# Four layers of graph network on one core: the second attention step's propagation two tile pairs at a time, and two reorderings in layer 0

## The chip, the cores and the metric

The kernel runs on one core of a Trainium2 chip. The metric is the device time of one execution in microseconds; lower is better. A core has a matrix engine (TensorE, PE in the profile, with PEld for its weight loads), VectorE (DVE), ScalarE (ACT), GpSimd (POOL) and SyncE (SP), which here issues most of the transfers between main memory and the on-chip memory. All engines run side by side, each through its own queue in order, and wait for one another on semaphores. TensorE reads the on-chip memory and writes accumulators (PSUM), from which VectorE and ScalarE copy.

## The reference

A graph of 3327 nodes with 256 features passes four residual layers. Cut to what matters:

```python
h = relu(layernorm(x)); x = x + adj @ (h @ W.T + b)                  # layer 0
h = relu(layernorm(x)); x = x + relu(filtered(adj) @ (tanh(h @ Wp + bp) @ Wg) + bg)   # layer 1
h = relu(layernorm(x)); x = x + relu(A_norm @ (h @ W.T))             # layer 2, A_norm from adj + I
h = relu(layernorm(x))                                               # layer 3
R = (adj + I) / rowsum;  Z = 0;  Xf = Xa = h
for n in range(2):
    A  = top_p_attention(Xa)      # softmax(q k^T), kept up to mass 0.9 in each row, renormalized
    Xf = R @ Xf                   # propagation
    Xa = A @ Xa                   # attention
    Z  = Z + Xf @ U1[n].T + Xa @ U2[n].T
x = x + layernorm(h + Z) * g + b
```

In layer 1, `filtered` is tanh of adj times adj where adj is positive (the reference keeps the 700 largest of a row; the kernel counts the positives and has a second path for rows with more). All arithmetic is float32.

## The kernel before

The nodes are padded to 26 tiles of 128 (T = 26, H = 13). Tile m of the lower half has a partner m + 13 in the upper half; the two are a *pair*. Each product with the adjacency matrix is done by a scheme with seven half-size products in place of eight: the matrix is seen as four quadrants of 13 x 13 tiles, and sums of quadrants (some kept in `s_dram` from layer 0 or 2) are multiplied with sums of blocks of the right side (`ts`, made by `combine_nodes` or `combine` on VectorE). The products are numbered 1 to 7; each takes 13 matmuls for a tile pair, and the results are added up to the four quarters of the pair's rows.

Layer 0 makes one pair at a time (`products`, `Product`): 91 matmuls with the matrix tile as the standing operand, then `Product.result` adds up. That needs one copy by ScalarE (L699) and six additions by VectorE (L705 to L710); the last of them sets the accumulator free. Layers 1 and 2 make two pairs at a time (`doubles`, `Double`): the right side stands, and the two tiles' matrix blocks stream through, 256 columns at a time. A double keeps two accumulator tiles (tag `row`, two buffers in all), so the first double of layer 1 needs the tile of layer 0's last pair. `Feed` loads matrix slabs and, on VectorE, makes the sums of quadrants; in layer 1 each slab is filtered first by `filtered` (on VectorE and ScalarE, for every fourth slab on ScalarE alone: L925, L926, L927).

When a pair of layer 0 is done, `finish0` makes its rows of x1 and stores them, and a `Pair` of layer 1 normalizes them (`measure`, `apply`), has TensorE transpose them (`turn`) and multiplies them by the weights (`hidden`). These steps are hung as hooks between the matmuls of the next pair; for the last pair, between those of the first double, at its matmuls 36 and 48 of 91.

The first rows of the kernel (`first_two_in`) are normalized while the input arrives. VectorE, ScalarE and SP are ordered by hand there: pairs 0 and 1 are measured, pair 0 applied, pair 2 measured, pair 1 applied, and so on.

Layer 3 goes by tiles. For each tile, the logits (`logits_steps`, L1233) go from the `row` accumulators through ScalarE's exponential (L1258) into a row of 3328 scores; VectorE and ScalarE search the threshold (`search_steps`: two passes on ScalarE, L1291 and L1296, and on VectorE L1301 to L1346, of which L1307 and L1344 are passes over all 3328 scores), and TensorE multiplies the masked row with the values (`rows_times_steps`: 26 transposes L223, copied by ScalarE at L226, and 26 matmuls L234). The search runs three tiles ahead (AHEAD = 3). Between two attentions TensorE runs a part of the propagation. In the first step these parts are doubles of four phases (`FirstPropagation`, products (1, 2), (5, 4), (6, 3), (7)). In the second step, after the tile pair (0, 13), they are the two phases of a pair (`PropagatedPair`): products 1, 2, 5, 4 and then 6, 7, 3, with the matrix block standing and 128 columns of the right side streaming (L1559). The outcome has nodes on the partitions, as the rows of the output need. `half` copies the first accumulator on ScalarE, `whole` does five additions on VectorE (L1579 to L1586), and `finish_pair` makes the output rows of both tiles: loads of `z`, `u` and `x3`, adds on POOL, the layer norm on VectorE with its root on POOL (L123, L125), three more adds on POOL. Their stores are issued during the next pair. The last pair, tiles 12 and 25, ends the kernel by `finish3` and `finish_last`, in which product 3 of tile 12 comes last.

TensorE's order is the order of the program. For the other engines a planner sorts the instructions at build time by its own estimates, within the dependencies; `tc.high_priority()` puts work ahead, and `tc.issue_after(x)` puts a block's instructions of x's engine behind x. In layer 3, `plan` says after which matmul of the phase (counted in 26ths) other work of TensorE is put in: the logits at 7, the transposes that begin the next attention at 20.

## Time and profile before

| what | us |
|---|---|
| time, median of 3 runs (2452.27 to 2454.14) | 2453.4 |
| the profiled execution: time, span | 2453.7, 2451.7 |
| TensorE busy (matmul), of the span | 2435.4 (99%) |
| TensorE weight loads busy | 2108.2 (86%) |
| VectorE busy | 2053.3 (84%) |
| ScalarE, POOL busy | 1112.3, 289.9 |
| layer 3's second attention step | about 1735 to 2442 |

A line of the groups gives the program line, the engine, the operation, out<-in by the program's names, the shape, the count, then the busy time of the group, the mean of one in ns, and the idle time of the engine before it with what ended it. Lines of the order of time begin with the start in us and the duration; a run of equal instructions is one line with its count. In the windows, each engine has its busy time and the number of its instructions.

A matmul's record is longer than the distance to the next, because matmuls are pipelined; the distance between starts is what a run of them costs.

### The profile page before, as it was taken

Reading aid. Unit: us, or ns where it says so; the run is one execution under the profiler, and the core shown is the slowest. Engines: PE = TensorE matmul, PEld = TensorE weight load, DVE = VectorE, ACT = ScalarE, POOL = GpSimd, SP = SyncE. Lnnn points to the kernel's source line nnn. Section 1 sums busy time; section 2 is a strip of 40 time slices with the busy share of each in tenths; the row PEclk is TensorE's granted clock in tenths of the full one; section 3 lists DMA queues with packets and bytes.
Section 4 is the critical chain, followed back from the end, with each engine's and each line's share of the span. In section 5 each row is a group of like instructions: output and inputs, shape, how many; then the busy total and the mean of one; then the engine's idle time right before and its main releaser. Section 6 shows DMA issues by size and latency. Waiting matters only on the chain. (4 is left out here: it accounts for less than half of the span.)

```text
span 2451.7 us, 41088 instructions
## 1 busy us (share of the span) xinstructions
PE 2435.4 (99%) x14475; PEld 2108.2 (86%) x14475; DVE 2053.3 (84%) x5280; ACT 1112.3 (45%) x2141; POOL 289.9 (12%) x462
## 2 busy tenths in 40 slices
PE   9999999999999999999999999999999999999998
PEld 8999988889888897777787778778888888888887
DVE  7877798788867768889788787985999999999995
ACT  3000045564011126656556565654556555655551
POOL 2000010000000100000000100000213222222222
PEclk9999999999999999999999999999999999999999
DMA  6788856566978666322332323333534433444343
GB/s 208 248 272 272 289 178 182 179 199 188 296 238 268 201 196 189 118 80 84 108 105 80 97 86 110 92 92 121 164 97 138 146 116 116 135 139 132 116 130 123
DMA packets 278674, 387.79 MB, mean 158 GB/s; under 512 B 24253, under 2 KB 216250, under 8 KB 278458
## 3 DMA queue, kind: packets, MB, share of 16 engines
q1 hardware_dynamic: 257322, 367.54, 48.3%
q10 hardware_dynamic: 21136, 17.52, 2.2%
q8 instruction: 116, 1.90, 0.3%
q14 instruction: 100, 0.82, 0.1%
HBM read 315.37 MB, written 67.89 MB: 156 GB/s over the span
## 5 line engine op out<-in xcount | busy, mean ns | idle before, releaser
L226 ACT COPY eT_a<-pt_a 128x512 f32<-128x512 f32 (+1 forms) x364 | 187.0, 557 | 366.6 <-PE pt_a L223 362.7
L234 PE MATMUL a<-h3a,eT_a 128*128 128x256 f32 x1352 | 311.7, 379 | 0.2 <-ACT eT_a L226 0.2
L234 PE MATMUL a<-vs,eT_a 128*128 128x256 f32 x1352 | 309.1, 379 | 0.2 <-ACT eT_a L226 0.2
L1320 DVE MAX8 cand_a<-w 128x8 f32<-128x128 f32 x1352 | 284.8, 278 | 4.0
L234 PEld LDWEIGHTS a<-h3a,eT_a 128*128 128x128 f32 x1352 | 249.5, 189 | 44.7 <-issue 10.1
L234 PEld LDWEIGHTS a<-vs,eT_a 128*128 128x128 f32 x1352 | 248.9, 190 | 30.1 <-ACT eT_a L226 0.5
L1316 DVE SCALAR_TENSOR_TENSOR w<-e_a,t_a 128x896 f32<-128x896 f32 x208 | 230.0, 1106 | 3.4
L1258 ACT ACTIVATE e_a<-pl_a 128x1024 f32<-128x1024 f32 x260 | 184.4, 729 | 37.2 <-PE pl_a L1233 36.8
L1307 DVE SCALAR_TENSOR_TENSOR w<-e_a,t_a 128x3328 uint8<-128x3328 f32 x52 | 192.0, 3692 | 4.6 <-DVE t_a L1304 0.5
L1344 DVE SCALAR_TENSOR_TENSOR e_a<-e_a,all_least 128x3328 f32<-128x3328 f32 x50 | 184.4, 3688 | 1.7
L223 PE MATMUL pt_a<-ident,e_a 128*128 128x128 f32 x1352 | 181.4, 272 | 0.0
L223 PEld LDWEIGHTS pt_a<-ident,e_a 128*128 128x128 f32 x1352 | 159.9, 141 | 19.1 <-issue 0.4
L777 PE MATMUL acc_a<-s_a,tsa 128*128 128x256 f32 (+1 forms) x728 | 169.0, 364 | 1.8 <-DVE y_a L710 1.8
L777 PE MATMUL acc_a<-a_a,tsa 128*128 128x256 f32 (+1 forms) x728 | 169.3, 365 | 0.0
L1500 PE MATMUL f0a<-slab3a_0a,tsa 128*128 128x256 f32 (+1 forms) x728 | 161.4, 367 | 0.3 <-DMA slab3a_0a<-s_dram 0.3
L1291 ACT ACTIVATE junk_a<-e_a,t_a 128x3328 uint8<-128x3328 f32 x52 | 159.7, 3071 | 0.5
L777 PE MATMUL acc_a<-a_a,rhs 128*128 128x256 f32 (+1 forms) x728 | 158.2, 364 | 0.0
L1296 ACT ACTIVATE junk_a<-e_a,t_a 128x3328 uint8<-128x3328 f32 x50 | 153.3, 3066 | 0.0
L1559 PE MATMUL f1a<-tsa,slab3a_1a 128*128 128x128 f32 x1248 | 148.1, 276 | 0.0
L777 PEld LDWEIGHTS acc_a<-s_a,tsa 128*128 128x128 f32 x728 | 130.6, 190 | 18.1 <-ACT a_a L927 2.2
L1559 PEld LDWEIGHTS f1a<-tsa,slab3a_1a 128*128 128x128 f32 x1248 | 144.0, 192 | 1.8
L1500 PEld LDWEIGHTS f0a<-slab3a_0a,tsa 128*128 128x128 f32 x728 | 126.7, 190 | 20.0 <-issue 3.8
(286 smaller groups left out, 4313.3 us busy)
## 6 DMA issues: line engine op xcount, KB each, us to landing
a_a<-in_adj_t_dram SPq DMA_DIRECT2D x216, 256.0 KB, 3.5
a_a<-in_adj_t_dram SPq DMA_DIRECT2D x144, 384.0 KB, 4.1
slab3a_0a<-s_dram SPq DMA_DIRECT2D x95, 384.0 KB, 4.0
slab3a_0a<-in_adj_t_dram SPq DMA_DIRECT2D x65, 384.0 KB, 4.0
slab3a_1a<-s_dram SPq DMA_DIRECT2D x60, 384.0 KB, 4.0
a_a<-in_adj_t_dram SPq DMA_DIRECT2D x60, 320.0 KB, 4.4
slab3a_1a<-in_adj_t_dram SPq DMA_DIRECT2D x48, 384.0 KB, 4.0
s_dram<-s_a SPq DMA_DIRECT2D x45, 256.0 KB, 4.4
```

Source lines behind the costliest of these rows:

```text
L223: nc.tensor.transpose(pt[:, j, :], e[:, k * P : (k + 1) * P], ident)
L226: last_turned.append(nc.scalar.copy(eT[:, : len(blocks), :], pt[:, : len(blocks), :]))
L234: nc.tensor.matmul(acc[:, :width], ready[g][:, j, :], rhs[:, k, :], start=(k == 0), stop=(k == T - 1))
L777: nc.tensor.matmul(self.acc[n], t, slab[:, :, k - cuts(self.many)[c][0], :], start=(k == 0 and n in (1, 5, 6, 7)), stop=(k == H - 1 and n ...
L1258: last_exp.append(nc.scalar.activation(dst, src, AF.Exp, accum_out=parts[:, c : c + 1]))
L1291: nc.scalar.activation(junk_a, e, AF.Relu, scale=-1.0, bias=t, accum_out=short)
L1307: nc.vector.scalar_tensor_tensor(junk, e, t, e, ALU.is_lt, ALU.mult, accum_out=got)
L1316: nc.vector.scalar_tensor_tensor(w[:, : (b - a) * P], eg, t, eg, ALU.is_lt, ALU.mult, accum_out=below[:, g : g + 1])
L1320: nc.vector.max(cand[:, 8 * k : 8 * k + 8], w[:, (k - a) * P : (k - a + 1) * P])
L1344: nc.vector.scalar_tensor_tensor(e, e, least, e, ALU.is_ge, ALU.mult, accum_out=kept)
L1500: nc.tensor.matmul(self.acc[:, self.at[n]], right_half(h3, ts, n, k), self.block(phase, at), start=not at, stop=at == len(units) - 1, skip ...
L1559: nc.tensor.matmul(self.accs[bank][:, c * P : (c + 1) * P], self.block(phase, at)[:, 0, :], right_half(self.h, self.ts, n, k), start=start ...
```

## The change

1. **Second step's propagation.** `PropagatedPair` goes; `SecondPropagation`, a subclass of `FirstPropagation`, takes its place for tiles 1 to 12 and 14 to 25: six doubles (tiles 1 and 2 with 14 and 15, and so on) of four phases, one behind each of four attentions. The attention order is now 0, 13, then 1, 2, 14, 15, 3, 4, 16, 17, ... The right side stands and 256 columns stream. The outcome has features on the partitions, so `turned` lets TensorE transpose it back, four transposes for two tiles, into a `row` accumulator, which VectorE reads directly (`rows`). `finish_two` replaces `finish_pair` and `finish_last`: it ends two tiles of the same half at a time. The lower two are begun (loads, POOL adds) in the third phase at 14 and turned in the fourth at 4; the upper two are begun in the next double's first phase at 4 and turned at 14. Stores are issued at 2 of a phase. In the short fourth phase (13 matmuls) the logits stand at 14 and the next attention's beginning at 22.
2. **The last double.** Its lower tiles 11 and 12 are turned and ended during the last attention. Product 7 of the upper tiles is made last with the matrix block standing, so that its outcome needs no turning: tile 25 first, then tile 24. All else of these tiles is turned and added before.
3. **Seam of layers 0 and 1.** For the last pair of layer 0 the second `combine_nodes` comes behind the six additions and the row sums. `finish0`, `measure` and `apply` of that pair move from there to matmul 10 of the first double, with its store, and lose their priority; `turn` moves from 36 to 44 and `hidden` from 48 to 56. ScalarE's filter of the fourth slab of the second group is put behind the copy L699. In layer 1's first double two further combinations are put behind the additions.
4. **First rows.** Pair 1 is applied before pair 2 is measured.

`xa` tiles get four buffers instead of two. The diff, cut to its core:

```diff
-                        self.change(s, (i, j) == QUADS[-1])
+                        with tc.issue_after(copied[-1].ins) if (p, c, i, j) == (0, 1, *QUADS[-1]) else nullcontext():
+                            self.change(s, (i, j) == QUADS[-1])
...
-                    if p == H - 1 and c:
-                        combine_nodes(following, *CUTS[c - 1])
+                    if p == H - 1 and c == 1:
+                        combine_nodes(following, *CUTS[0])
...
-                with tc.high_priority() if p == H - 1 else nullcontext():
-                    finish(p, x2, y, p3)
-                    pair = pair_after(p, x2)
+                row_sums(p, p3)
+                if p == H - 1:
+                    with tc.issue_after(summed_up[-1].ins):
+                        combine_nodes(following, *CUTS[1])
+                    made = []
+
+                    def last():
+                        finish(p, x2, y)
+                        made.append(pair_after(p, x2))
+
+                    return [last, lambda: made[0].turn(), lambda: made[0].hidden()]
...
                 pairs[0].apply()
+                pairs[1].apply()
                 pairs[2].measure()
-                pairs[1].apply()
...
-                finish1, left, (36, 48), ((26, 36), (14, 20)), second_layer, following=rhs2,
+                finish1, left, (10, 44, 56), ((26, 36), (14, 20)), second_layer, following=rhs2,
...
+        class SecondPropagation(FirstPropagation):
+            def __init__(self, d):
+                super().__init__(d)
+                self.p, self.many, self.width, self.phases = 2 * d + 1, 2, 2 * P, OF_DOUBLE
+                self.h, self.name = fs[0], f"1{tag}_{d}"
+                self.last = d == DOUBLES - 1
...
             def steps(self, phase):
+                if not self.last or phase < len(self.phases) - 1:
+                    yield from super().steps(phase)
+                    return
+                self.sevens = [new_acc(f"f{self.name}_7")[:, :P], new_acc(f"f{self.name}_8")[:, :P]]
+                for done, t in enumerate((1, 0)):
+                    for at, (n, k) in enumerate(units):
+                        nc.tensor.matmul(
+                            self.sevens[t], self.block(phase, at)[:, t, :], right_half(self.h, ts, n, k),
+                            start=not at, stop=at == len(units) - 1,
+                        )
+                        yield done * len(units) + at
+
+            def turned(self, i):
+                acc = one_bank(f"ft{self.name}_{i}")
+                for t in range(2):
+                    for j in range(NC):
+                        at = t * D + j * P
+                        nc.tensor.transpose(acc[:, at : at + P], self.ys[i][:, j, t * P : (t + 1) * P], ident)
+                return [acc[:, t * D : (t + 1) * D] for t in range(2)]
...
+        def finish_two(prop, i, room=None):
...
+            with tc.issue_after(prop.loaded.ins):
+                for t, m in enumerate(ms):
...
+                    nc.sync.dma_start(zs[-1], z_dram[:, m, :])
+                x3s, us = shares(name, *enumerate(ms), room=room)
...
+            def rows():
+                for t, (m, row) in enumerate(zip(ms, prop.turned(i))):
+                    with tc.high_priority():
+                        nc.vector.scalar_tensor_tensor(zs[t], row, rinv[:, m : m + 1], zs[t], ALU.mult, ALU.add)
...
+            def end():
...
+                for t, m in ((1, ms[1]), (0, ms[0])):
...
+                        nc.vector.scalar_tensor_tensor(
+                            halves_of_z, seven, rinv[:, m : m + 1], halves_of_z, ALU.mult, ALU.add
+                        )
...
-        ORDER = [p + i * H for p in range(H) for i in range(2)]
+        ORDER = [0, H] + [p + t + i * H for p in range(1, H, 2) for i in range(2) for t in range(2)]
...
-                plan = whole_run(prepare(1, ahead, kT1), 7) if ahead else {}
+                short = i >= 2 and i % 4 == 1
+                plan = whole_run(prepare(1, ahead, kT1), 14 if short else 7) if ahead else {}
                 if i + 1 < T:
-                    plan = merged(plan, {20: [lambda: rows.begin(ORDER[i + 1])]}, later)
+                    plan = merged(plan, {22 if short else 20: [lambda: rows.begin(ORDER[i + 1])]}, later)
...
+                    last = i + 1 == T
+                    plan = merged(plan, {2: [functools.partial(stores_of_last, prop)]})
+                    if phase == 2:
+                        plan = merged(plan, {14: [functools.partial(begin, prop, 0)]})
+                    elif phase == 3:
+                        plan = plan if last else merged(plan, {4: [turn]})
+                    elif phase == 0 and d:
+                        plan = merged(plan, {4: [functools.partial(begin, before, 1)], 14: [turn]})
...
+                    if last:
+                        at_end = finish_two(prop, 1, ep.tile([P, NP], F32, tag="e", name=f"room{tag}"))
+                        plan = merged(plan, {6: [at_end[0]]})
+                    run(prop.steps(phase), {int(k * units // T): v for k, v in plan.items()})
+                    if last:
+                        at_end[2]()
```

## The prediction, as put on record

> **What bounds the kernel now.** I read the 40 slices first, then the second attention step's window, then the order of time at the three places that the change touches.
>
> ```profile
> PE   9999999999999999999999999999999999999998
> ...
> DVE  7877798788867768889788787985999999999995
> ```
> ```profile
> core 0: us, PE busy (x) PEld busy (x) DVE busy (x) ACT busy (x) POOL busy (x), PEclk, DMA share, GB/s
> ...
> 1806.00:2400.00 594.00, 594.00 (x4023) 527.04 (x4023) 565.05 (x1621) 335.60 (x627) 148.76 (x198) 1.00 0.44 131
> ```
>
> TensorE never rests between its first matmul and 2441.78 us, at full clock: a microsecond taken from its order of work is a microsecond of the kernel, unless something else makes it wait. The second row says what that could be: in the second step VectorE is busy 565 of 594 us. Its waits there add up to 31 us, of which 17.4 us belong to the last iteration, and between instructions it mostly loses 0.04 us. Both engines take 54.85 us for two tiles (the attention masks of L1344 begin at 2030.41, 2085.3, 2140.2), so VectorE has nearly no room either.
>
> TensorE's price is the step from one start to the next, read from unbroken runs in the order of time:
>
> ```profile
> 2372.75 1.04 PE L223 MATMUL pt_a<-ident,e_a 128*128 128x128 f32 x8
> 2373.62 3.62 PE L234 MATMUL a<-vs,eT_a 128*128 128x256 f32 x16
> ...
> 2384.22 5.97 PE L1559 MATMUL f1a<-tsa,slab3a_1a 128*128 128x128 f32 x52
> ```
>
> Every float32 matmul is two records. Narrow: (5.97 - 0.275) / 51 = 0.1117 us a record. Wide: (3.62 - 0.379) / 15 = 0.2161. A transpose is one record: (1.04 - 0.272) / 7 = 0.109.
>
> **The change part by part.** The sum is made against the profiled execution, 2453.7 us with a span of 2451.7; the median of the three runs, 2453.4, is 0.3 below, and the difference is applied to the median.
>
> *Propagation in doubles.* Before: 12 pairs x 91 matmuls x 2 = 2184 narrow records (1248 + 936 in the groups of L1559). After: 6 doubles x 91 x 2 = 1092 wide ones, but the last double's product 7 (13 matmuls, 26 records) becomes 52 narrow: 1066 wide and 52 narrow. 2184 x 0.1117 = 244.0; 1066 x 0.2161 + 52 x 0.1117 = 236.2: **-7.7 us**, 7.3 ns for each pair of narrow records. The other end is the groups' busy time, which counts each run's trailing end:
>
> ```profile
> L1500 PE MATMUL f0a<-slab3a_0a,tsa 128*128 128x256 f32 x624 | 148.7, 382 | 0.3 <-DMA slab3a_0a<-s_dram 0.3
> L1559 PE MATMUL f1a<-tsa,slab3a_1a 128*128 128x128 f32 x1248 | 148.1, 276 | 0.0
> L1559 PE MATMUL f1a<-fsa,slab3a_1a 128*128 128x128 f32 x936 | 113.1, 276 | 0.0
> ```
>
> 261.2 / 2184 = 119.6 ns narrow, 148.7 / 624 = 238.3 wide: 0.9 ns a pair, -1.0 us. I take -7.7, since starts are what the sequence pays.
>
> The page "TensorE: Matmul & The Clock Gate" of the Trainium skill, section "Back-to-back issue gap", says that in a stream of weight loads and matmuls a 128-column matmul takes some 81 ns where the isolated gap would be 56. By that, halving their number would save 25 ns a pair, an estimate of 27 us in place of 7.7; the starts above show 7.3 ns a pair, and the row decides. The forecast would be 2430.4 by the page, 2449.7 by the rows.
>
> *Turning back.* The wide product has features on the partitions, so each double pays 4 transposes per group of two tiles: 6 x 2 x 4 = 48 x 0.109 = **+5.2 us**. The worst row is the pairs of L183, 10.3 us for 52: 0.198, +9.5.
>
> *VectorE, ScalarE, POOL, SP in the step.* Per four tiles, `whole` twice (starts 0.20, 0.20, 0.33, 0.19, 0.33 apart: 2.5 us) gives way to `keep`, two operations of 512 columns at 0.6 (as L804) and three of 256 at 0.33: 2.2 us. ScalarE's two copies of 512 stay two. POOL's adds stay, but tiles 11 and 24 trade two POOL operations each for one more on VectorE. SP's six loads and two stores per two tiles stay in number. For tiles 13 places up (`i` = 1) they move to the start of the next double's first phase, right behind the stores that must free the two `z` buffers. Stores issued 1.8 us into the phase land 4.2 later, six issues take 6 x 0.43: SP is held until about 8.6, with slab loads queued behind. Six slabs of three units cover 6 x 1.3 us plus 3.1 us of logits and 0.44 of transposes, 11.3 us; slab 7 would land at 8.6 + 4.0, 1.3 late unless it slips ahead. I take 0, ends 0 and +1.3 in each of five doubles. POOL's four adds (0.73 each) would end at 8.6 + 3.1 + 2.9 = 14.6, while VectorE comes to these rows 3.4 to 6.8 after the transposes' end at 9.5: it may wait 1.7, and TensorE only through the masks (rival C).
>
> *The short phase (product 7 alone, 5.6 us).* Here the new waits are. After two units TensorE transposes two tiles into one of two row buffers; at unit 7 the next tile's logits want both. Cover: five units (2.2) and the first chunk (0.9), 3.1 us. VectorE must by then have run two operations of 0.4. How late it comes to such work is seen at L1618, which frees the same buffers in the first step:
>
> ```profile
> 1132.41 1.88 PE L1611 MATMUL u<-u2s,xT_a 128*128 128x512 f32 x4
> ...
> 1137.70 0.42 DVE L1618 TENSOR_TENSOR z<-u,h3a 128x256 f32<-128x256 f32 x1
> ```
>
> 3.4 us after the product's end at 1134.29; over that step 3.4 to 6.8, except the last two. With 0.8 for the two operations that is 4.2 to 7.6, a wait of 1.1 to 4.5. The lower end is 0: in the second step the mask of L1344 (2054.88, 3.69 long) begins just as a phase does (2055.1), so the two reads would stand right behind it at 3.8 to 4.4, and ScalarE's exponentials could free the other buffer at 5.1. Also ScalarE may still be at the exponentials' small operations when the early transposes of the next attention want copying (0 to 0.6). The new phase's place against the mask is nearest to the second reading: I take 0.3 in each of five, **+1.5 us**, ends 0 and +23.
>
> The page "Perfetto Trace Analysis", section "Optimization Strategy", says that a bubble which repeats on the saturated engine can mean too little PSUM or SBUF for the next tile. It speaks against a further user of the two row buffers; no row of before has such a bubble there, and the sum does not use it.
>
> *The end.* Before, the last product ends at 2441.78 and VectorE finishes two tiles in turn:
>
> ```profile
> 2443.66 0.20 DVE L1708 BATCH_NORM_AGGREGATE mv<-st 128x2 f32<-128x12 f32 x1
> ...
> 2444.89 0.48 DVE L1712 SCALAR_TENSOR_TENSOR z<-z,r,x 128x256 f32<-128x256 f32 x1 [0.45 <-POOL r L125]
> 2445.80 0.60 SPq L1713 DMA_DIRECT2D out_dram<-z  x1
> ```
>
> 3.6 us to the end of L1712, with the aggregate 0.7 behind its statistics because the other tile stands between. After, tile 25's product is complete 26 x 0.112 = 2.9 us before tile 24's, and its chain is nearly through. Tile 24's: 0.2 + 0.50 + 0.45 + 0.20 + 0.20 + 0.75 + 0.05 + 0.48 = 2.85. **-0.5 us**, ends -0.75 and +0.2 (the other chain's last operation in between). Its first product needs a second accumulator, perhaps the one that ScalarE still reads (L1752: 0.1 + 0.47 after the attention): **+0.2**, ends 0 and +0.6.
>
> *Seam of layers 0 and 1.*
>
> ```profile
> 332.26 0.46 ACT L699 COPY p_a<-acc_a 128x387 f32<-128x387 f32 x1
> ...
> 335.72 0.28 DVE L710 TENSOR_TENSOR y_a<-u_a,acc_a 128x128 f32<-128x128 f32 x1
> ...
> 336.14 1.53 PE L777 MATMUL acc_a<-s_a,tsa 128*128 128x256 f32 x6 [1.78 <-DVE y_a L710]
> ```
>
> TensorE ended product 12 at 329.0, but the copy stood behind filter operations of a later slab, and VectorE's reads behind four combinations of 0.6. The change puts three filter operations (0.84 each; behind them ScalarE's tanh of the third slab group) and the four combinations (2.7 us; behind them the second group's sums and pair 12's finish) after them: the copy near 330.6, the last read near 333.5, before the 334.2 at which TensorE asks. What is late next: the combinations, wanted at step 27 (340.7, ready about 338.5); pair 12's finish, now at step 10 of the double with its store on ScalarE's queue, wanted turned at step 44 (348.0, ready about 346.4); its hidden product at step 56, through at 361 for step 77 (364.4). **-1.8 us**, ends -1.95 and 0.
>
> *First rows.*
>
> ```profile
> 7.27 0.43 DVE L416 BATCH_NORM_STATS2 st_a<-rhs 128x6 f32<-128x256 f32 x1 [0.75 <-DMA rhs<-in_x_dram]
> ...
> 8.34 0.75 PE L445 MATMUL pt_a<-ident,xn_a 128*128 128x128 f32 x4 [0.67 <-DVE xn_a L433]
> ```
>
> Pair 1's scaling waited behind pair 2's statistics, hence for a load; its root was there at 6.84. Swapped, it runs at 6.9 instead of 7.88, and ScalarE's eviction of pair 0 comes 0.9 earlier. Pair 2's root is then due at 9.4, its scaled rows at 10.3, where TensorE would want them at 10.06 and had them at 10.96: **-0.6 us**, ends -0.9 and 0. TensorE runs gapless from 9.13 on, so it lasts.
>
> Sum: -7.7 + 5.2 + 1.5 - 0.5 + 0.2 - 1.8 - 0.6 = **-3.7 us**, 2449.7.
>
> **The rivals.** A. *No new wait anywhere*, the masks covering the turned rows: -7.7 + 5.2 - 0.75 - 1.95 - 0.9 = -6.1, 2447.3. For it: masks begin with the phase. Against: the 3.4 us at L1618.
> B. *Slower: the logits of the short phase wait for VectorE*, by L1618's lag. At its middle, 2.8 us in each of five, 14 instead of 1.5: +8.8, 2462.2. It decides from 2.0 us a phase, (5.2 + 4.9) / 5. Against: a longer TensorE period gives VectorE time to catch up.
> C. *VectorE is the bound of the second step*, so the 2.5 us saved there (7.7 - 5.2) and the 1.5 both vanish: -2.7, 2450.7. For it: equal periods; against: its own 0.3 us less per four tiles.
> D. *The seam's wait comes back* at step 44 or 77: -1.9, 2451.5.
> E. *Wide records aren't cheaper*, as busy time has it, so the change doesn't do what it says: -3.7 + 6.7 = +3.0, 2456.4.
>
> **How the numbers follow.** Forecast 0.33, A 0.27, B 0.18, C 0.10, D 0.06, E 0.06. A measurement tells 0.2%, 4.9 us, from no change. Faster: A and a quarter of the forecast, whose own range is 2447.5 to 2452: 0.36. Slower: most of B, some of E: 0.19. Same: 0.45. The range 2446.3 to 2460 leaves out the best of A (0.07) and what of B lies over 2.4 us a phase (0.11).
>
> **What would show it.** Wide records of the second step 0.216 apart; no wait at the old 334; the second transposes of pairs at 7.7 instead of 8.34; 3 us from the last product to the last VectorE operation. Wrong if TensorE idles before logits in every fourth tile (B), if masks come late for the transposes of L223 (C), or if L445 or L777 wait near 348 or 364 (D).

## The result, and the profile after

The changed kernel takes 2478.0 us (median of 5 runs, 2477.1 to 2480.8), the kernel before beside it 2453.5. The ratio is 1.0102, with a 95% interval of 1.0091 to 1.0113: 24.5 us slower. The forecast was 2449.7 with a range up to 2460, so it is wrong in sign and outside its range. The profiled execution took 2477.7 us, with a span of 2475.4.

The 40 slices hardly tell: TensorE looks as full as before.

```profile
PE   9999999999999999999999999999999999999998
...
DVE  7887798788767759889787887986998988989995
```

The window on the second attention step, with the same columns as before, says where to look. TensorE was busy for all 594.00 us of it and is now busy for 573.58. VectorE, the engine that I had feared as the next bound, has got idler too (565.05 to 538.01), and the mean granted clock (the share of TensorE's full clock that the profile shows as granted) is 0.99.

```profile
core 0: us, PE busy (x) PEld busy (x) DVE busy (x) ACT busy (x) POOL busy (x), PEclk, DMA share, GB/s
1806.00:2400.00 594.00, 573.58 (x2930) 473.62 (x2929) 538.01 (x1527) 325.56 (x616) 128.30 (x182) 0.99 0.42 125
```

TensorE's waits between 1740 and 2460 us (columns: total, times, longest) are of one kind, and there were none in this stretch before:

```profile
engine line waited for: us in total, times, longest us
PE a L234 <- ACT eT_a L226: 20.4, 10, 4.6
```

The attention's products (L234) wait for ScalarE's copies of the turned masks (L226). What ScalarE waits for in turn stands in the page's groups, where the last column is the idle time just before the group and what ended it:

```profile
L234 PE MATMUL a<-vs,eT_a 128*128 128x256 f32 x1352 | 316.1, 385 | 20.7 <-ACT eT_a L226 20.7
...
L1306 ACT ACTIVATE junk_a<-e_a,t_a 128x3328 uint8<-128x3328 f32 x52 | 159.7, 3072 | 25.2 <-POOL e_a L1259 24.7
```

L1259 is POOL's zeroing of one column: a tile's 3327 scores are padded to 3328, and the last column is set to 0 before ScalarE's Relu pass (L1306) reads the row. It takes 0.1 us, and ScalarE stood 24.7 us for it. In the kernel before, the same pass in the same stretch had no idle time before it:

```profile
L1291 ACT ACTIVATE junk_a<-e_a,t_a 128x3328 uint8<-128x3328 f32 x24 | 73.7, 3072 | 0.0
```

The order of time shows one of the five places, the attention behind the last phase of the first double. (Lines of the other work are left out.)

```profile
1898.52 4.12 DVE L1322 SCALAR_TENSOR_TENSOR w<-e_a,t_a 128x3328 uint8<-128x3328 f32 x1
...
1899.12 4.11 POOL L1737 TENSOR_TENSOR z<-z,u1s 128x256 f32<-128x256 f32 x1
...
1901.90 0.29 ACT L1295 ACTIVATE t_a<-mean_a,lnv_a 128x1 f32<-128x1 f32 x1
1902.10 1.05 ACT L226 COPY eT_a<-pt_a 128x512 f32<-128x512 f32 x2
...
1902.72 1.99 PE L234 MATMUL a<-vs,eT_a 128*128 128x256 f32 x8 [0.83 <-ACT eT_a L226]
...
1903.94 2.57 SPq L1721 DMA_DIRECT2D out_dram<-z  x2
...
1904.67 1.46 POOL L1739 TENSOR_TENSOR z<-z,x_1a 128x256 f32<-128x256 f32 x1
...
1907.58 0.85 SPq L1705 DMA_DIRECT2D z<-z_dram  x2
...
1910.14 1.56 POOL L1708 TENSOR_TENSOR z<-z,u_1a 128x256 f32<-128x256 f32 x1 [4.01 <-DMA z<-z_dram]
...
1912.44 0.10 POOL L1259 MEMSET e_a<- 128x1 f32 x1
...
1912.58 3.07 ACT L1306 ACTIVATE junk_a<-e_a,t_a 128x3328 uint8<-128x3328 f32 x1 [6.31 <-POOL e_a L1259]
...
1915.64 1.05 ACT L226 COPY eT_a<-pt_a 128x512 f32<-128x512 f32 x2
...
1916.26 1.22 PE L234 MATMUL a<-vs,eT_a 128*128 128x256 f32 x2 [4.62 <-ACT eT_a L226]
```

Read from below, it is a chain through five queues. TensorE wants a copy; the copy stands in ScalarE's queue behind the Relu pass; the pass waits for the zeroing; the zeroing stands in POOL's queue behind z+u (L1708), which begins the next two tiles; that add waits 4.01 us for a load of z; the load waits for a `z` buffer, which the two stores of the tiles before must free; and the stores wait for POOL's own last adds of their norm (L1737 to L1739), one of which, an L1737, was held for 4.11 us beside a pass of VectorE. A smaller wait stands above: when the attention begins, ScalarE has only just ended the small operations behind the exponentials (L1295), so the first copies come 0.83 us late.

There are five such attentions, one behind the short fourth phase of each of the doubles 0 to 4. Against the usual distance of the records, TensorE loses 0.99 to 1.00 us at the start of each, and 4.78, 4.36, 2.63, 3.00 and 2.30 us within: 22.1 us together. Another 5.5 us go behind the first three, where the granted clock falls to a half (last section).

### The profile page after: what moved, and what is told of

Read it like the earlier page. It is cut to its first block, busy times and chain, and to the rows that moved or that the text cites. A ratio compares the mean times of both kernels' runs of the same rounds, so it can differ in the third digit from the quotient of the medians.

```text
span 2475.4 us, 38987 instructions
## 1 busy us (share of the span) xinstructions
PE 2441.5 (99%) x13457; PEld 2075.9 (84%) x13457; DVE 2052.0 (83%) x5252; ACT 1114.1 (45%) x2141; POOL 280.4 (11%) x457
## 4 chain that ended last, share of the span: by engine, by line
PE 93%; DMA 2%; POOL 2%; issue 2%; DVE 1%; ACT 0%; SPq 0%; POOLq 0%; DVEq 0%; ACTq 0%
PE a L234 23%; PE acc_a L789 21%; PE acc_a L684 11%; PE f0a L1512 10%; PE f1a L1512 9%; PE pl_a L1248 6%; PE pt_a L223 5%; PE out_a L823 2%; PE u L1632 2%; PE u L1613 2%; PE prj_a L457 1%; PE f L1416 1%; PE pt_a L445 1%; PE pkq_a L290 0%; PE pkq L290 0%
## 5 line engine op out<-in xcount | busy, mean ns | idle before, releaser
L226 ACT COPY eT_a<-pt_a 128x512 f32<-128x512 f32 (+1 forms) x364 | 187.1, 557 | 359.1 <-PE pt_a L223 354.9
L234 PE MATMUL a<-vs,eT_a 128*128 128x256 f32 x1352 | 316.1, 385 | 20.7 <-ACT eT_a L226 20.7
L234 PE MATMUL a<-h3a,eT_a 128*128 128x256 f32 x1352 | 311.7, 379 | 0.2 <-ACT eT_a L226 0.2
L234 PEld LDWEIGHTS a<-vs,eT_a 128*128 128x128 f32 x1352 | 253.2, 193 | 56.4 <-ACT eT_a L226 24.9
L234 PEld LDWEIGHTS a<-h3a,eT_a 128*128 128x128 f32 x1352 | 249.5, 189 | 44.7 <-issue 10.1
L1331 DVE SCALAR_TENSOR_TENSOR w<-e_a,t_a 128x896 f32<-128x896 f32 x208 | 228.7, 1100 | 3.6
L1322 DVE SCALAR_TENSOR_TENSOR w<-e_a,t_a 128x3328 uint8<-128x3328 f32 x52 | 194.0, 3731 | 4.2
L1359 DVE SCALAR_TENSOR_TENSOR e_a<-e_a,all_least 128x3328 f32<-128x3328 f32 x50 | 184.4, 3688 | 1.8
L1306 ACT ACTIVATE junk_a<-e_a,t_a 128x3328 uint8<-128x3328 f32 x52 | 159.7, 3072 | 25.2 <-POOL e_a L1259 24.7
L789 PE MATMUL acc_a<-s_a,tsa 128*128 128x256 f32 (+1 forms) x728 | 168.8, 364 | 1.0 <-ACT a_a L938 1.0
L789 PE MATMUL acc_a<-a_a,tsa 128*128 128x256 f32 (+1 forms) x728 | 169.3, 365 | 0.0
L789 PE MATMUL acc_a<-a_a,rhs 128*128 128x256 f32 (+1 forms) x728 | 158.4, 364 | 0.0
L789 PEld LDWEIGHTS acc_a<-s_a,tsa 128*128 128x128 f32 x728 | 130.6, 190 | 17.4 <-ACT a_a L938 1.4
L789 PEld LDWEIGHTS acc_a<-a_a,tsa 128*128 128x128 f32 x728 | 130.3, 190 | 15.6
L789 PEld LDWEIGHTS acc_a<-a_a,rhs 128*128 128x128 f32 x728 | 130.0, 190 | 15.9 <-ACT y_a L811 0.2
```

The costliest lines, as they stand in the source:

```text
L226: last_turned.append(nc.scalar.copy(eT[:, : len(blocks), :], pt[:, : len(blocks), :]))
L234: nc.tensor.matmul(acc[:, :width], ready[g][:, j, :], rhs[:, k, :], start=(k == 0), stop=(k == T - 1))
L789: nc.tensor.matmul(self.acc[n], t, slab[:, :, k - cuts(self.many)[c][0], :], start=(k == 0 and n in (1, 5, 6, 7)), stop=(k == H - 1 and n ...
L1306: nc.scalar.activation(junk_a, e, AF.Relu, scale=-1.0, bias=t, accum_out=short)
L1322: nc.vector.scalar_tensor_tensor(junk, e, t, e, ALU.is_lt, ALU.mult, accum_out=got)
L1331: nc.vector.scalar_tensor_tensor(w[:, : (b - a) * P], eg, t, eg, ALU.is_lt, ALU.mult, accum_out=below[:, g : g + 1])
```

## The experiments

Theory 1: POOL's order holds the zeroing, and through it ScalarE and TensorE; the late logits of the short phase add the 1.0 us at each start. Theory 2: VectorE, or the turned rows that it must read (the forecast's rivals B and C), is late, and ScalarE only passes that on. Theory 3: the late logits alone crowd ScalarE and cause all of it. A run's time stands against the kernel before on the same chip: 2452.8 us for the first four runs, 2453.2 for the next four, 2453.9 for the last three.

| run | edit | median us | ratio to before (95%) |
|---|---|---|---|
| order | changed kernel, POOL's adds behind the zeroing | 2453.8 | 1.0003 (0.9994 to 1.0012) |
| own_room | changed kernel, own room for the second half's z | 2454.0 | 1.0002 (0.9993 to 1.0011) |
| pad_act | changed kernel, zeroing on ScalarE | 2460.4 | 1.0030 (1.0018 to 1.0042) |
| early | changed kernel, logits at 7, begin at 20 | 2449.3 | 0.9984 (0.9975 to 0.9993) |
| logits7_begin22 | order, and logits at 7 | 2449.5 | 0.9981 (0.9972 to 0.9990) |
| logits14_begin20 | order, and begin at 20 | 2453.6 | 0.9999 (0.9990 to 1.0009) |
| seam_first | before, with parts 3 and 4 alone | 2451.5 | 0.9995 (0.9986 to 1.0004) |
| doubles_early | before, with parts 1 and 2, logits at 7, begin at 20 | 2451.1 | 0.9991 (0.9982 to 1.0000) |
| no_turn | early, without the 48 transposes | 2445.7 | 0.9969 (0.9958 to 0.9980) |
| stores_late | early, one pair's stores asked for later | 2449.7 | 0.9985 (0.9976 to 0.9994) |
| early_room | early and own_room together | 2449.5 | 0.9981 (0.9972 to 0.9990) |

**order: only POOL's order.**

```diff
-            nc.gpsimd.memset(e[:, N:], 0.0)
+            pad_zeroed[:] = [nc.gpsimd.memset(e[:, N:], 0.0)]
...
-            for t, m in enumerate(ms):
-                nc.gpsimd.tensor_tensor(zs[t], zs[t], us[:, t, :], ALU.add)
-                nc.gpsimd.tensor_tensor(zs[t], zs[t], ys.pop(m), ALU.add)
+            with tc.issue_after(pad_zeroed[-1].ins):
+                for t, m in enumerate(ms):
+                    nc.gpsimd.tensor_tensor(zs[t], zs[t], us[:, t, :], ALU.add)
+                    nc.gpsimd.tensor_tensor(zs[t], zs[t], ys.pop(m), ALU.add)
```

> The changed kernel, with one order added on POOL: the four adds that begin a half of a double (z+u, z+y) may not be put ahead of the zeroing of the last column of the scores' tile that was written before them in the program. Nothing else differs. In the changed kernel's trace the zeroing stands at 1912.44 us behind an add that waited 4.0 us for a load, and ScalarE's Relu pass and the copies of the turned masks wait behind it; TensorE loses 27.7 us in this way, about 1.0 us at the start of each of five attentions and 2.3 to 4.8 us within it, and some echoes. Theory 1 (POOL's order is the cause of the waits within the attention): the zeroing comes some 7 us earlier, right behind the norms' adds (about 1905.4), the inside waits of 17 us and their echoes go, the five waits of 1.0 us at the start stay: 2455 to 2462 us. Theory 2 (VectorE, or the rows turned back, are late and ScalarE merely passes it on): nothing moves, 2478 us. Theory 3 (ScalarE is crowded since the logits of every fourth stretch come late, at 14 of 26): the waits within the attention stay, 2474 to 2478 us.

2453.8 us, 24.2 below the changed kernel (23.5 when each is taken against its own kernel before) and a little better than theory 1 asked. Its order of time, at the same place:

```profile
1902.76 1.46 POOL L1740 TENSOR_TENSOR z<-z,x_1a 128x256 f32<-128x256 f32 x1
...
1904.16 0.10 POOL L1259 MEMSET e_a<- 128x1 f32 x1
1904.37 3.07 ACT L1306 ACTIVATE junk_a<-e_a,t_a 128x3328 uint8<-128x3328 f32 x1
...
1907.88 2.12 POOL L1709 TENSOR_TENSOR z<-z,u_1a 128x256 f32<-128x256 f32 x2 [3.63 <-DMA z<-z_dram]
```

POOL waits for the same load as before (3.63 us), but nobody stands behind it any more: the zeroing comes right after the norm's adds. (Lines behind the edit are one higher: L1709 here is L1708 above.) What is left of TensorE's waits for ScalarE is 4.1 us in five, the starts of the attentions. Theories 2 and 3, which expected 2474 us or more, fall as the main cause: VectorE, the turned rows and the late logits are all as they were.

**own_room: the same chain cut further up.** The second half's two z get room in the weights `u1s`, of which that piece is no longer read. So their loads need not wait for stores.

```diff
-                        w3.tile([P, D], F32, tag="z", name=f"z1_{m}") if room is None else room[:, t * D : (t + 1) * D]
+                        room[:, t * D : (t + 1) * D] if room is not None
+                        else u1s[:, 1, t, :] if i else w3.tile([P, D], F32, tag="z", name=f"z1_{m}")
```

> The changed kernel, with room of its own for the second half's two sums (a piece of the weights that is no longer read), so that their loads need not wait until the first half's two results have been stored. The late logits, the zeroing on POOL and the program's order stay; what POOL does first is planned anew, and the adds may come earlier for it. Theory 1, with its whole chain (zeroing behind adds, adds behind loads, loads behind stores): POOL no longer stands 4.0 us before the adds, the zeroing comes as early as when it is put ahead of the adds, and what is left are the five waits of 1.0 us: 2454 to 2458 us. If the loads are late for another reason (SP's queue, the transfers before them) POOL still waits 2 to 4 us: 2465 to 2478 us.

2454.0 us. The order of POOL and the zeroing is not fixed here, the loads alone are free; the planner now puts the adds ahead of the norms, into time in which POOL had been idle, and the zeroing comes as early as in the run before:

```profile
1891.78 1.22 POOL L1710 TENSOR_TENSOR u1s<-u1s,y 128x256 f32<-128x256 f32 x1 [6.98 <-ACT y L1767]
...
1898.39 4.11 POOL L1738 TENSOR_TENSOR z<-z,u1s 128x256 f32<-128x256 f32 x1
...
1905.35 0.10 POOL L1259 MEMSET e_a<- 128x1 f32 x1
...
1905.51 3.07 ACT L1306 ACTIVATE junk_a<-e_a,t_a 128x3328 uint8<-128x3328 f32 x1
```

The POOL add of 4.11 us is still there and costs TensorE nothing. So the buffers that the loads had to wait for are a link of the chain, and the long add alone is not enough to make the wait. Since the planner moved the adds as well, the run shows the free loads and the earlier adds together.

**pad_act: POOL out of it.**

```diff
-            nc.gpsimd.memset(e[:, N:], 0.0)
+            nc.scalar.activation(e[:, N:], tiny, AF.Copy, scale=0.0)
```

> The changed kernel, with the last column of the scores' tile zeroed by ScalarE (one column, a Copy by 0) right behind its exponentials, and no longer by POOL. POOL keeps all its adds, in whatever order. Theory 1: ScalarE's Relu pass never waits for POOL, so the waits within the five attentions go as they do when POOL is reordered, or a little more: 2452 to 2462 us; ScalarE gets 26 more instructions of about 0.2 us, which lie beside TensorE's work except in the five late stretches (at most +1 us). Theory 2 (VectorE or the turned rows): 2478 us. Theory 3 (late logits): 2474 to 2478 us, since the exponentials end where they did.

2460.4 us: 17.6 of the 24 are gone, and the time lies inside the expected 2452 to 2462, but 6.5 above `order`. The waits show why:

```profile
PE a L234 <- ACT eT_a L226: 4.8, 6, 0.9
PE pt_a L223 <- DVE all_target L1297: 3.7, 1, 3.7
```

In the second step only the five starts are left, as in `order`, each 0.09 us longer. The 3.7 us are a new wait at 957 us, in the first attention step, whose order the planner changed too; behind it the granted clock is 0.57 between 961 and 965. Why VectorE's small operation stands late there was not followed up.

**early, logits7_begin22, logits14_begin20: the late logits.**

```diff
-                plan = whole_run(prepare(1, ahead, kT1), 14 if short else 7) if ahead else {}
+                plan = whole_run(prepare(1, ahead, kT1), 7) if ahead else {}
...
-                    plan = merged(plan, {22 if short else 20: [lambda: rows.begin(ORDER[i + 1])]}, later)
+                    plan = merged(plan, {20: [lambda: rows.begin(ORDER[i + 1])]}, later)
```

> The changed kernel, with the logits of every fourth stretch back at 7 of 26 (as in all the others) and the next attention's first part back at 20, in place of 14 and 22. The order of POOL changes with it: the zeroing is now planned ahead of the next half's adds. Theory 1 and theory 3 both expect the waits of 1.0 us at the start and those within the attention to go: 2449 to 2456 us. Theory 2, and my forecast's rival B (the logits wait for VectorE's read of the turned rows, since both use the row buffers): a new wait before the logits of every fourth stretch, 1 to 2 us each, so 5 to 10 us of the gain are lost, or, if this was the cause all along, 2478 us or more.

2449.3 us: both kinds of wait are gone. The planner, too, puts the zeroing ahead of the adds once the exponentials come earlier, so this run alone would not have told theory 1 from theory 3; `order` does. The window of the second step is nearly full again:

```profile
1806.00:2400.00 594.00, 593.10 (x3073) 494.81 (x3072) 562.45 (x1596) 335.24 (x628) 133.88 (x194) 1.00 0.43 132
```

Rival B's wait, at the logits of the short phase, does not appear. (In the profile of `logits7_begin22` it stands once, at 2002.99, with 0.25 us.) The two further runs have POOL's order mended and one half of the edit each.

> The changed kernel with POOL's order mended (the zeroing ahead of the adds: 2453.8 us, where five waits of 1.0 us were left at the start of the attention behind every fourth stretch), and now the logits of that stretch at 7 of 26, the next attention's first part left at 22. If the five waits are ScalarE's, which still has the late exponentials and their small operations before it when the first masks want copying, they go: 2449 us. If they come of the first part being begun late, they stay: 2454 us.

> The same with the other half of the edit: the logits left at 14 of 26, the next attention's first part at 20. If the five waits of 1.0 us come of the late exponentials on ScalarE, they stay: 2454 us. If they come of the first part being begun late, they go: 2449 us. Both half: 2451 us each.

2449.5 and 2453.6 us. With the logits at 7 the five waits are gone. With only the begin at 20 they are five still; they are shorter in the view of waits, but the time shows no gain:

```profile
PE a L234 <- ACT eT_a L226: 2.5, 5, 0.5
```

So the 1.0 us at each start comes of the late exponentials on ScalarE: 4.1 us in all by these two runs, 4.5 by `order` and `early`.

**seam_first, doubles_early: the parts apart.** `seam_first` is the kernel before with the diff's hunks up to layer 2; `doubles_early` has the rest of the diff and the edit of `early`.

> The kernel before, with the change's third and fourth parts alone: the seam of layers 0 and 1, and the order of the first rows. By the forecast -1.8 and -0.6 us, together -2.4: 2451.1 us. By the trace of the changed kernel the seam's wait only shrank from 1.95 to 1.19 us and the first rows were 0.1 us ahead by 329 us: 2452.6 us, about -0.9 us.

> The kernel before, with the change's first and second parts alone (the propagation in doubles and the last double's early tiles), and with the early logits, so that none of the new waits stands in the way. By the forecast's terms -7.7 + 5.2 - 0.5 + 0.2 = -2.8 us: about 2450.0 us; by the difference of the runs with early logits and with the last two parts alone (2449.3 and 2451.45) -2.15: 2450.7 us. If the wide propagation saved nothing: 2453 to 2456 us.

2451.5 and 2451.1 us, 1.4 and 2.1 below the kernel before; `early`, which has both, is 3.5 below. The first interval includes no change and the second ends at it, so each part alone is only about a microsecond from what can be told; the sum agrees with both.

**no_turn: the transposes.** `early` without them; VectorE reads the sums where `keep` left them, so the rows of 24 tiles are not the reference's.

```diff
-                acc = one_bank(f"ft{self.name}_{i}")
-                for t in range(2):
-                    for j in range(NC):
-                        at = t * D + j * P
-                        nc.tensor.transpose(acc[:, at : at + P], self.ys[i][:, j, t * P : (t + 1) * P], ident)
-                return [acc[:, t * D : (t + 1) * D] for t in range(2)]
+                return [self.ys[i][:, :, t * P : (t + 1) * P] for t in range(2)]
```

> The version with the early logits (2449.3 us), without the 48 transposes that turn the doubles' sums back into rows: VectorE reads the sums as they are, so the results of 24 tiles are not the reference's. It measures the term of +5.2 us (48 by 0.108 us) of the forecast by itself. If the transposes cost their rows and nothing hangs on them: 5.2 us less, 2444.1 us. If each step of four also costs TensorE a stand before or behind it, 0.1 us by 12 more: 2443 us. If they lay in the shade of other work: 2449 us.

2445.7 us (2443.7 to 2449.1): 3.6 less than `early`, or 4.0 when each is taken against its own kernel before, and not 5.2. In the trace of `early` four transposes take 0.436 to 0.437 us from the first one's start to the start of the next product, twelve times: 5.2 us, 0.109 each, as forecast. Without them 1.9 us are given back in the logits of the short phase, whose 16 records take 3.38 us in place of 3.00, five times.

**stores_late: the last wait of early.** In `early` one wait is left in the second step, 0.9 us at 2391, for POOL's addition of the identity to a slab, of the kind of L1451.

```diff
-                    plan = merged(plan, {2: [functools.partial(stores_of_last, prop)]})
+                    plan = merged(plan, {20 if phase == 1 else 2: [functools.partial(stores_of_last, prop)]})
```

> The version with the early logits, with the stores of the second half issued at 20 of 26 of the stretch behind, in place of 2. In that version's trace TensorE waits once more, 0.9 us at 2391, for an identity add on POOL whose slab SP could only load behind two stores that had waited for the norms' adds. If SP's order is the reason, that wait goes: 2448.3 us, with no other change; if the add's own length is (3.66 us beside a pass of VectorE), it stays: 2449.3 us.

2449.7 us, and the wait is 0.8. In the trace the two stores have moved behind one slab load only (2382.57), ahead of the others, so the edit hardly did what it was meant to and does not tell the two reasons apart. What can be seen is that the add takes 3.25 us, beginning under a pass of VectorE (3.66 in `early`), and that in both runs it ends 0.31 us behind that pass, whenever it began.

**early_room.**

> The early logits (2449.3 us) together with the room of its own for the second half's sums. POOL's order no longer matters with the early logits, so by theory 1 the room gives nothing more there; the wait of 0.9 us at 2391, for an identity add on POOL that runs beside a pass of VectorE, may shift by half a us either way: 2449 us, 2448 to 2450.

2449.5 us, with 0.7 us of waits in the second step: nothing more to gain, as theory 1 has it. `early`, `early_room` and `logits7_begin22` are faster than both kernels, by 3.5 to 4.4 us against the kernel before; the simplest is `early`, two numbers away from the changed kernel.

## Why the prediction was wrong

**The step that failed** is the pair of paragraphs on the other engines and on the short phase, whose terms were 0 and +1.5; together they measured +28.7 (2478.0 less 2449.3; 28.0 when each is taken against its own kernel before). The first said of SP's held queue "I take 0", and of POOL's four adds that VectorE "may wait 1.7, and TensorE only through the masks". The loads behind the stores were seen, and the adds behind the loads; what stands behind the adds on POOL was not asked. It is the zeroing of a column, which I had listed nowhere because nothing waited for it in the trace of before. Nor did the adds run where the program has them, in the next double's first phase: SP and POOL follow the planner, and it had put them into the attention ahead of that phase. By `order` this is 24.2 us, not all of it waits: 17.1 us within the attentions, 5.5 us of half clock behind three of them, and some 1.6 us that also lie between two profiles (the seam's wait is 1.0 us in the one and absent in the other).

**The late logits.** "ScalarE may still be at the exponentials' small operations", with 0 to 0.6 us, named the mechanism. It measured 1.0 us at each of the five starts and 4.1 to 4.5 in the runs, where the 1.5 had been put down for VectorE.

**The rivals.** B, the only rival on the slow side, named the right phase and a wrong place: in the profile of after there is no wait before the logits, and VectorE's rows cost nothing. C did not come about; VectorE's busy time fell with TensorE's. D did not either: no L445 or L789 wait stands near 348 or 364. E falls with the groups below.

**The wide propagation**, forecast -7.7, and the transposes, +5.2. The view by line has the records that the sum counted:

```profile
L1512 PE MATMUL f1a<-slab3a_1a,tsa 128*128 128x256 f32 x598 | 138.5, 382 | 0.0
...
L1512 PE MATMUL f1a<-slab3a_1a,fsa 128*128 128x256 f32 x468 | 107.4, 380 | 0.0
...
L1588 PE MATMUL ft1a<-ident,y_1a 128*128 128x128 f32 x48 | 7.2, 273 | 0.0
...
L1576 PE MATMUL f1a<-tsa,slab3a_1a 128*128 128x128 f32 x52 | 6.4, 276 | 0.0
```

598 + 468 is the 1066 wide records, and they start 0.216 us apart, as in the sum. Added up from each start to the next, the second step's propagation by doubles or pairs takes 247.9 us in `seam_first` and 241.3 in `early`, of which 1.1 are the wait at 2391: the wide form saves 7.7. The transposes take the 5.2 shown above, so both terms were right. Of their -2.5 the runs have about -2.1 (`early` against `seam_first`, and `doubles_early` against the kernel before), with that wait and part 2's end in it.

**The end**, -0.5 and +0.2. TensorE's last matmul ends at 2467.0:

```profile
2462.61 4.41 PE L1576 MATMUL f1a<-tsa,slab3a_1a 128*128 128x128 f32 x38
...
2469.25 0.48 DVE L1758 SCALAR_TENSOR_TENSOR rooma<-rooma,r_1a 128x256 f32<-128x256 f32 x1 [0.45 <-POOL r_1a L125]
```

From there to the end of VectorE's last operation it is 2.7 us, 3.6 before: -0.9, and no wait at L1576 for the second accumulator. The last transfer is 0.6 us quicker as well (5.7 us from that operation to the span's end, 6.3 before). The forecast had -0.3, with 2.85 us for tile 24's chain (its terms add up to 2.83); the part was better than forecast.

**The seam**, -1.8. ScalarE's copy came at 330.53 as forecast (330.6), but VectorE's last read at 334.86 and not at 333.5:

```profile
333.60 0.28 DVE L708 TENSOR_TENSOR u_a<-p_a,acc_a 128x128 f32<-128x128 f32 x1
...
334.86 0.29 DVE L713 TENSOR_TENSOR y_a<-u_a,acc_a 128x128 f32<-128x128 f32 x1
```

Between copy and reads VectorE still ran 2.6 us of sums and a filter operation for the slabs, which the forecast did not put down. Nor is VectorE's read all that TensorE waits for: the view names ScalarE's filter (L938) wherever a wait is left with this part, and in the profile of after that filter ends 0.01 us behind the read. The eleven profiles with this part wait 0 to 1.7 us at this place, 0.4 in the mean; the two without it, of the kernel before and of `doubles_early`, 1.8 and 1.1. So about 1 us is saved, not 1.8, and one profile of it tells little. What makes it differ from run to run stays open.

**The first rows**, -0.6. The second transposes came at 7.45 and the projection at 7.88:

```profile
7.45 0.60 PE L445 MATMUL pt_a<-ident,xn_a 128*128 128x128 f32 x4
7.88 1.89 PE L457 MATMUL prj_a<-w0s,xT_a 128*128 128x256 f32 x8
```

That was earlier than forecast (7.7 for the transposes), but "TensorE runs gapless from 9.13 on, so it lasts" was wrong: with the earlier start new gaps of 0.18 to 0.28 us appeared at 10.2, 12.6 and 23.7, where the products wait for ScalarE's copies of the turned rows (L449). In the profile of after 0.1 us was left. Other profiles with this part differ: the projection came at 8.79 in `seam_first` and at 8.77 in `early`, there behind a load of its weights. Both parts together are 1.4 us by `seam_first`, and 1.4 again by `early` less `doubles_early`, each against its own kernel before; the forecast had 2.4.

**The sum without the new waits** was -3.7 - 1.5 = -5.2; `early` measures -3.5. That the forecast's 2449.7 is its time to 0.4 us is thus partly luck. Its opening, that TensorE "never rests" between its first matmul and 2441.78, was too strong as well: it was busy for 2435.4 of those 2440.2 us, with no wait in the second step but 1.78 at the seam.

## What to carry to other kernels

When work moves onto an engine with a queue of its own, list what already stands in that queue behind the new place, the smallest instructions first, and who waits for each: a fill of 0.1 us set the time here, and in the trace of before it showed no wait. Where a planner orders the other engines, the place in the program does not say where an instruction runs; work that waits for a load can be put by it ahead of work that others need, as here, unless an explicit order forbids that. Of a chain of such links it is enough to cut one: an order, a buffer, or the place of the work ahead each gave the time back.

## What the runs showed of the hardware

**POOL stands while VectorE passes over two operands.** An add of 256 columns on POOL takes 0.72 to 0.74 us in 105 of 122 cases in the profile of after. All five that began under the full pass L1322 took 4.10 to 4.11 us in the profile of after, and ended 0.58 to 0.59 us behind the pass; an add of 128 columns (0.45 us otherwise) ended 0.31 behind it. Two under the pass L1359 took 3.05 and 3.98 us, and ten under shorter operations of VectorE, eight of them the passes L1331, 1.17 to 1.56, among them the L1739 and the L1708 shown above. Under the searches for the largest (L1340) the adds kept their 0.73. In the other direction, the pass shown above began during an add of POOL (L1738, 1898.43 to 1899.15) and took 4.12 us in place of 3.69. The page "SBUF — State Buffer" of the Trainium skill, section "SBUF: two separate sides", states a lock between the two engines, held for a whole instruction, for VectorE's operations with two inputs in the memory; the rows agree with it, in both directions. It lengthened the chain by 3.4 us, but `own_room`, in which the add of 4.11 us stays, shows that by itself it cost TensorE nothing.

**A wait of TensorE can be paid for again behind it.** After the wait of 4.78 us the granted clock was 0.50 for 3.5 us:

```profile
1905.50:1909.00 3.50, 3.50 (x19) 3.04 (x19) 3.46 (x16) 0.76 (x2) 0.63 (x1) 1.00 0.42 124
1911.50:1916.20 4.70, 0.14 (x1) 0.00 (x0) 4.63 (x21) 3.62 (x4) 3.00 (x6) 0.75 0.46 154
1916.30:1919.80 3.50, 3.50 (x8) 2.71 (x9) 3.22 (x12) 0.40 (x1) 0.00 (x0) 0.50 0.00 0
```

8 records of 256 columns fill 3.5 us there; before the wait 3.5 us held 19, most of them of 256 columns. The records behind the waits of 4.78, 4.36 and 2.63 us lost 5.5 us together, 0.21 for each of 256 columns; behind the waits of 3.00 and 2.30 none did, and behind the one of 2.63 it began 1.4 us late. So the length of the wait alone does not decide it. In the trace's clock records the half clock starts at 1913.85, 2033.32 and 2149.37 and lasts 6.83, 3.41 and 3.41 us; the starts lie 35 and 34 times 3.41 us apart. In this trace the clock thus changes only at steps of 3.41 us, and the first change fell inside the wait; that a wait's place against these steps decides what it costs fits these rows, but no run here tests it. The page "TensorE: Matmul & The Clock Gate", section "HAM oscillation — how this bites in real kernels", gives as a rule no gaps above about 3.4 us; the half clock behind 2.63 us is outside it.
